# Normalising attention weights in the product that turns them, instead of before a transpose

## The chip, the cores and the metric

The kernel runs on one core of one Trainium2 chip. The metric is the device time of one execution in microseconds (us), from the median of several runs. A profile of one execution is shown beside it. Engine names in the profile are: PE for TensorE (PEld for its weight loads), DVE for VectorE, ACT for ScalarE, POOL for GpSimd, SP for SyncE.

## The reference

The reference is a two-layer model on 64 samples of 32 latent tokens with 256 channels, each sample with a context of 257 rows of 256 channels, all in float32. A layer is a cross attention to the context, a self attention and a feed-forward part (the first layer's is a mixture of 64 experts). The change touches the softmax of the two cross attentions alone. Cut to that:

```python
# layer 0: 16 heads, keys are the 257 context rows and the sample's own 32 tokens
sim  = einsum('bhid,bhjd->bhij', qn, kn)          # j runs over 289 keys
attn = softmax(where(mask, sim, -max), axis=-1)
out  = einsum('bhij,bhjd->bhid', attn, v)
x    = x + out.reshape(b, m, h * d) @ Wout + bout

# layer 1: 16 heads, keys are the 257 context rows
attn = softmax(einsum('bqhd,bkhd->bhqk', q, k), axis=-1)
y    = einsum('bhqk,bkhd->bqhd', attn, v)
x    = x + einsum('bqhd,hdo->bqo', y, wo) + bo
```

A softmax row is exp(s - max) divided by the sum of its exponentials. The division by the sum is what the change moves.

## The kernel before, in words

**Tiling.** The 2048 tokens are 16 tiles of 128 tokens, a tile holds four samples. In both cross attentions one sample has 32 tokens x 16 heads = 512 query rows, kept as four groups (g) of 128 rows on the partitions: `sim` is a tile of 128 x 4 x keys.

**Stages.** `before` runs the first cross attention, the self attention and the routing. `experts` runs the mixture. `after` runs the second cross attention, self attention and feed-forward part. In `before` and `after` a loop goes over the 64 samples, and one pass is called a slot here. The order of TensorE is the order of the program (`manual_schedule` for PE); the other engines are ordered by a scheduler that follows priorities, and `urgent` raises the priority of what is in it. In a slot the loop does one step of each of several samples, and generators (`tails`, `fronts`, `steps`) fill in the work of token tiles between them.

**First cross attention** (class CrossFirst). A slot does `keys(s + 2)`, `weigh(s)`, `norms(s + 2)`, `values(s)`, `spread(s + 2)`, `turn(s + 3)`, `scores(s + 2)` and `prepare(s + 4)`, with fill-in work at three places. `keys` multiplies 289 columns of the context by the key weights, 16 products with the name psA<-xT,wk. `norms` sums squares (line 1247, which reads the squares that ScalarE makes in line 1235). `scores` forms the query-key products (1287), multiplies them into `sim` (1297), adds the mask (1298) and calls `softmax_rows`: a maximum (193), four exponentials with their sums (195), a reciprocal of the sums (198), a scaled copy of the last 33 columns to a second place of the same tile (201), and the scaling of the four groups in place, two on ScalarE (206) and two on VectorE (208). The tile has three buffers, and behind the 289 columns it has room for that second copy.

**weigh.** `keyed` turns the weights: for each of three column groups of 128 keys it transposes the four row groups by TensorE into one PSUM bank (218) and copies the bank to SBUF (219), on whichever of ScalarE and VectorE the scheduler picks. `values` then multiplies the turned weights with the context (232, 242). Every transpose passes the 128x128 tile as the stationary operand and an identity from the constants tile `c` as the moving one, so the profile calls it psT<-c,sim.

**Second cross attention** (class CrossSecond). A slot does `weigh(s)`, `scores(s + 2)` and `values(s)`. `scores` has four products (psY<-xT,qk), each followed by a maximum (1387) and an exponential out of PSUM (1388), then a reciprocal (1391) and four scalings on VectorE (1393). `weigh` transposes two column groups and a third one in which key 256 is repeated 128 times (1405), and copies the banks out (1406). `values` multiplies with the context and adds the part of key 256 (1418).

**GpSimd's queue.** It has the two small copies into xT (1206, 1207) for `turn`, the scaling of queries (1151), the mask (1174, 1175), some additions, and the indirect transfers of the routing (665) and of the mixture's results (802). It works strictly in its own order.

Of the kernel before, what the change touches and what calls it, by code (L numbers as in the profile page):

```python
# [10 lines left out]
F32 = mybir.dt.float32  # L11
# [3 lines left out]
ALU = mybir.AluOpType  # L15
AX = mybir.AxisListType

P = 128
D = 256
S = 32  # L20
NB = P // S
J = 257
JK = J + S
# [76 lines left out]
class Kernel:  # L100
    def __init__(self, ctx, tc, a, out):
        self.ctx, self.tc, self.nc, self.a, self.out = ctx, tc, tc.nc, a, out
        self.nt = out.shape[0] // P
        self.nb = self.nt * NB
        self.const = ctx.enter_context(tc.tile_pool(name="const", bufs=1))
        self.ps = ctx.enter_context(tc.tile_pool(name="ps", bufs=8, space=bass.MemoryType.PSUM))
        self.small = ctx.enter_context(tc.tile_pool(name="small", bufs=4))
# [76 lines left out]
        nc.vector.tensor_tensor(xt, xt, ps, ALU.add)  # L184


    def softmax_rows(self, sim, n, twice=None):


        nc = self.nc  # L190
        mx = self.small.tile([P, 4], F32, name="mx")
        sm = self.small.tile([P, 4], F32, name="sm")
        nc.vector.tensor_reduce(mx, sim, AX.X, ALU.max, negate=True)  # L193
        for g in range(4):
            nc.scalar.activation(  # L195
                sim[:, g, :], sim[:, g, :], AF.Exp, bias=mx[:, g : g + 1], accum_out=sm[:, g : g + 1]
            )
        nc.vector.reciprocal(sm, sm)
        if twice is not None:
            m = twice.shape[2]  # L200
            nc.vector.tensor_tensor(
                twice, sim[:, :, n - m :], sm.unsqueeze(2).to_broadcast([P, 4, m]), ALU.mult
            )
        for g in range(4):
            if g % 2:
                nc.scalar.mul(sim[:, g, :], sim[:, g, :], sm[:, g : g + 1])
            else:
                nc.vector.tensor_scalar(sim[:, g, :], sim[:, g, :], sm[:, g : g + 1], None, ALU.mult)

    def keyed(self, sim, sizes):  # L210

        nc = self.nc
        at = self.atp.tile([P, len(sizes), 512], F32, name="at")
        k0 = 0
        for j, n in enumerate(sizes):
            ps = self.bank("psT")
            for g in range(4):
                nc.tensor.transpose(ps[:n, g * P : (g + 1) * P], sim[:, g, k0 : k0 + n], self.ident)
            nc.any.tensor_copy(at[:n, j, :], ps[:n, :])
            k0 += n  # L220
        return [at[:n, j, :] for j, n in enumerate(sizes)]
# [454 lines left out]
    def experts(self, ctx, slot, tails):  # L676
# [75 lines left out]
        for e in range(AHEAD):  # L752
            weigh(e)
# [17 lines left out]
        for e in range(E):  # L771
            weigh(e + AHEAD)
            fetch(e + 3)
            turn(e + 2)
            while (at - total + rest) * E < rest * e:
                next(side)
                at += 1
            inner(e + 1)
            outer(e)
            if e == AHEAD:  # L780
                self.after_weights()
            if e == 2 * AHEAD:
                self.ffnw = self.ffn_weights(self.w2)
# [319 lines left out]
class CrossFirst:  # L1103


    def __init__(self, k, kp):
        self.k, self.kp = k, kp
        self.own, self.held, self.cx, self.xT = {}, {}, {}, {}

    def given(self, wq, wk, gx, bx, gl, bl, gam, xl, xlT):  # L1110
        self.wq, self.wk_ = wq, wk
# [160 lines left out]
    def scores(self, s):  # L1272
        k = self.k
        nc = k.nc
        t, b = divmod(s, NB)
        _, _, qT, mb = self.own[t]
        _, _, kT, whole = self.held[s]
        sim = whole[:, :, :JK]
        for half in range(2):
            ps = [k.bank("psB") for _ in range(2)]  # L1280
            for u in range(2):
                for i in range(2):
                    for odd in range(2):
                        m = 2 * (2 * half + i) + u
                        q = PLACES[i].index(2 * u + odd)
                        r = slice(DH * odd, DH * odd + DH)
                        nc.tensor.matmul(
                            ps[i][q * S : (q + 1) * S, :JK],
                            lhsT=qT[r, m, b * S : (b + 1) * S],
                            rhs=kT[r, m, :],  # L1290
                            start=True,
                            stop=True,
                        )
            for i in range(2):
                g = 2 * half + i
                with k.urgent():
                    nc.vector.tensor_tensor(sim[:, g, :], ps[i][:, :JK], sim[:, g, :], ALU.mult)  # L1297
        nc.vector.tensor_tensor(sim, sim, mb[:, b, :].unsqueeze(1).to_broadcast([P, 4, JK]), ALU.add)
        k.softmax_rows(sim, JK, whole[:, :, 2 * P + 64 : 2 * P + 64 + S + 1])

    def weigh(self, s):

        k = self.k
        cx, c3, _, sim = self.held.pop(s)
        at = k.keyed(sim, [P, P, P])
        self.weights = at[:2], [cx[:, 0, :], cx[:, 1, :]], (at[2], c3)

    def values(self, s):
# [7 lines left out]
class CrossSecond:  # L1316
# [54 lines left out]
    def scores(self, s):  # L1371

        k, nc = self.k, self.k.nc
        t, b = divmod(s, NB)
        cx, xT = self.cx[s]
        qk = self.qk[t]
        sim = self.kp.tile([P, 4, J], F32, name="sim")
        mx = k.small.tile([P, 4], F32, name="mx")
        sm = k.small.tile([P, 4], F32, name="sm")
        for g in range(4):  # L1380
            ps = k.bank("psY")
            k.product(
                ps[:, :J],
                [qk[:, c, b, g * P : (g + 1) * P] for c in range(2)],
                [xT[:, c, :] for c in range(2)],
            )
            nc.vector.tensor_reduce(mx[:, g : g + 1], ps[:, :J], AX.X, ALU.max, negate=True)  # L1387
            nc.scalar.activation(  # L1388
                sim[:, g, :], ps[:, :J], AF.Exp, bias=mx[:, g : g + 1], accum_out=sm[:, g : g + 1]
            )  # L1390
        nc.vector.reciprocal(sm, sm)
        for g in range(4):
            nc.vector.tensor_scalar(sim[:, g, :], sim[:, g, :], sm[:, g : g + 1], None, ALU.mult)  # L1393
        self.held[s] = sim

    def weigh(self, s):

        k, nc = self.k, self.k.nc
        sim = self.held.pop(s)
        at = self.kp.tile([P, 3, 512], F32, name="at", bufs=1)  # L1400
        for j in range(3):
            ps = k.bank("psT")
            for g in range(4):
                x = sim[:, g, j * P : (j + 1) * P] if j < 2 else sim[:, g, J - 1 :].to_broadcast([P, P])
                nc.tensor.transpose(ps[:, g * P : (g + 1) * P], x, k.ident)  # L1405
            nc.any.tensor_copy(at[:, j, :], ps)
        self.at = at

# [93 lines left out]
```

## Time and profile before

| what | us |
|---|---|
| median of 3 timed runs | 2816.75 |
| lowest and highest of them | 2816.62, 2820.55 |
| the profiled execution's own time | 2814.6 |
| span of the profile, first to last instruction | 2812.4 |
| TensorE busy | 2650.2 |
| VectorE busy | 1730.6 |
| ScalarE busy | 1227.6 |
| GpSimd busy | 542.3 |

The busy times overlap, as the engines work side by side. A row of the profile's groups reads: line, engine, operation, what it writes and reads, shape, count, then the busy time of the group, the mean duration of one instruction in nanoseconds, and how long the engine sat idle before instructions of the group and what ended that. TensorE's matmuls are pipelined, so that the mean of one is longer than the distance from one start to the next. A row of the timeline has start, length, engine, line, operation and how many records it merges.

### The profile page before, as it was taken

The numbers are of one execution on the slowest core, as the hardware profiler recorded it, in microseconds if no ns is written. First come the engines' busy times: TensorE is split into PE (matmuls) and PEld (weight loads), VectorE is DVE, ScalarE is ACT, GpSimd is POOL, SyncE is SP. The second block draws the span as 40 slices with busy tenths as digits, with TensorE's granted clock in tenths as the row PEclk, the third lists the DMA queues.
The fourth block names the chain that finished last, engine by engine and source line by source line (L and its number), as shares of the span: only waits on it lengthen the run. The fifth ranks groups of instructions, "written<-read, shape, count | busy, mean of one in ns | idle before, by whom it ended". The sixth has DMA issues, their size and how long they took to land. (4 is left out here: it accounts for less than half of the span.)

```text
span 2812.4 us, 59421 instructions
## 1 busy us (share of the span) xinstructions
PE 2650.2 (94%) x23642; PEld 1823.7 (65%) x23642; DVE 1730.6 (62%) x4544; ACT 1227.6 (44%) x3463; POOL 542.3 (19%) x644
## 2 busy tenths in 40 slices
PE   6999999999999999999998799899999999999995
PEld 4566656665666566656665578677777777777763
DVE  6565656665666567656755433556666666666664
ACT  4555555555555555555553233333333333333331
POOL 3110122112211221122112200421222222121001
PEclk9999999999999999999998799999999999999997
DMA  7000011101100000000002587221212222221110
GB/s 263 27 16 14 18 31 33 31 18 31 32 30 18 27 26 22 18 19 19 17 5 82 182 268 229 80 71 48 61 48 58 52 55 59 50 57 47 33 33 7
DMA packets 136089, 157.05 MB, mean 56 GB/s; under 512 B 24025, under 2 KB 118980, under 8 KB 135813
## 3 DMA queue, kind: packets, MB, share of 16 engines
q1 hardware_dynamic: 114308, 119.65, 14.0%
q0 software_dynamic: 12288, 25.21, 3.4%
q10 hardware_dynamic: 9216, 8.39, 0.9%
q8 instruction: 187, 3.06, 0.5%
q14 instruction: 90, 0.73, 0.1%
HBM read 121.63 MB, written 37.75 MB: 57 GB/s over the span
## 5 line engine op out<-in xcount | busy, mean ns | idle before, releaser
L178 PE MATMUL psA<-xT,wk 128*128 128x289 f32 x2048 | 522.0, 410 | 17.9 <-issue 13.0
L178 PEld LDWEIGHTS psA<-xT,wk 128*128 128x128 f32 x2048 | 384.0, 190 | 150.1 <-issue 46.5
L802 POOL DMA_INDIRECT y<-oute,idx x128 | 131.5, 1027 | 657.4 <-DVE x L813 466.8
L232 PE MATMUL psY<-at,cx 128*128 128x512 f32 x512 | 238.1, 608 | 0.0
L178 PE MATMUL psA<-at,cx 128*128 128x512 f32 x512 | 233.5, 599 | 0.0
L178 PE MATMUL psY<-xT,qk 128*128 128x257 f32 x1024 | 233.5, 380 | 0.0
L178 PEld LDWEIGHTS psY<-xT,qk 128*128 128x128 f32 x1024 | 189.8, 190 | 25.1
L1388 ACT ACTIVATE sim<-psY,mx 128x257 f32<-128x257 f32 x256 | 120.8, 476 | 148.6 <-DVE mx L1387 147.7
L232 PEld LDWEIGHTS psY<-at,cx 128*128 128x128 f32 x512 | 92.8, 191 | 123.1 <-issue 99.7
L195 ACT ACTIVATE sim<-sim,mx 128x289 f32<-128x289 f32 x256 | 135.5, 532 | 64.4 <-DVE mx L193 64.3
L178 PEld LDWEIGHTS psA<-at,cx 128*128 128x128 f32 x512 | 93.4, 190 | 96.5 <-issue 83.3
L1235 ACT ACTIVATE sq<-kT 128x1156 f32<-128x1156 f32 x128 | 148.6, 1161 | 12.6 <-DVE kT L1232 11.4
L244 ACT COPY yT<-psY 128x512 f32<-128x512 f32 x128 | 68.7, 589 | 189.8 <-PE psY L242 189.8
L1297 DVE TENSOR_TENSOR sim<-psB,sim 128x289 f32<-128x289 f32 x256 | 100.7, 451 | 81.5 <-PE psA L178 37.9
L1230 ACT COPY kT<-psA 128x289 f32<-128x289 f32 x256 | 99.2, 388 | 115.7 <-PE psA L178 113.6
L665 POOL DMA_INDIRECT buf<-z,fi x128 | 126.4, 987 | 96.3 <-DVE fi L662 54.0
L1232 DVE COPY kT<-psA 128x289 f32<-128x289 f32 x256 | 114.3, 451 | 40.0 <-PE psA L178 39.9
L178 PE MATMUL psY<-yT,wv 128*64 128x128 f32 x2048 | 127.9, 277 | 7.3 <-DVE yT L1418 7.3
L1387 DVE TENSOR_REDUCE mx<-psY 128x1 f32<-128x257 f32 x256 | 101.0, 418 | 52.6 <-PE psY L178 47.5
L178 PEld LDWEIGHTS psY<-yT,wv 128*64 128x64 f32 x2048 | 116.6, 138 | 16.3 <-DVE yT L1418 11.2
L184 DVE TENSOR_TENSOR x<-x,psY 128x256 f32<-128x256 f32 (+1 forms) x80 | 29.2, 365 | 156.4 <-PE psY L178 154.8
L178 PE MATMUL psY<-wo,oT 128*128 128x128 f32 (+1 forms) x768 | 124.2, 315 | 0.0
(254 smaller groups left out, 5005.7 us busy)
## 6 DMA issues: line engine op xcount, KB each, us to landing
cx<-in_ctx SPq DMA_DIRECT2D x128, 256.0 KB
we<-in_m_ew SPq DMA_DIRECT2D x64, 384.0 KB
xT<-in_ctxT SPq DMA_DIRECT2D x64, 257.0 KB
buf<-zero SPq DMA_DIRECT2D x32, 256.0 KB
be<-buf SPq DMA_DIRECT2D x64, 128.0 KB
oute<-oe ACTq DMA_DIRECT2D x64, 128.0 KB
mu<-in_mask SPq DMA_DIRECT2D x16, 128.5 KB
x<-in_x SPq DMA_DIRECT2D x16, 128.0 KB
```

The lines of the kernel that those rows point to most:

```text
L178: self.nc.tensor.matmul(ps, lhsT=lhs[i], rhs=rhs[i], start=(i == 0), stop=(i == n - 1))
L195: nc.scalar.activation(sim[:, g, :], sim[:, g, :], AF.Exp, bias=mx[:, g : g + 1], accum_out=sm[:, g : g + 1])
L232: nc.tensor.matmul(ps[kc], lhsT=values[i][:, kc * P : (kc + 1) * P], rhs=at[i], start=(i == 0), stop=(i == n - 1 and tail is None),)
L244: nc.any.tensor_copy(yT[:, kc, :, b * S : (b + 1) * S], ps[kc].rearrange("p (h i) -> p h i", h=H))
L665: d = nc.gpsimd.indirect_dma_start(out=self.buf[:, :], out_offset=bass.IndirectOffsetOnAxis(ap=fi[:, k : k + 1], axis=0), in_=z[:, 0, :], ...
L802: nc.gpsimd.indirect_dma_start(out=y, out_offset=None, in_=self.oute[:, :], in_offset=bass.IndirectOffsetOnAxis(ap=self.idx[:, t, k : k + ...
L1230: nc.scalar.copy(kT[:, p, :], ps[:, :JK])
L1232: nc.vector.tensor_copy(kT[:, p, :], ps[:, :JK])
L1235: nc.scalar.activation(sq[p // 4], kT[:, p - 3 : p + 1, :], AF.Square)
L1297: nc.vector.tensor_tensor(sim[:, g, :], ps[i][:, :JK], sim[:, g, :], ALU.mult)
L1387: nc.vector.tensor_reduce(mx[:, g : g + 1], ps[:, :J], AX.X, ALU.max, negate=True)
L1388: nc.scalar.activation(sim[:, g, :], ps[:, :J], AF.Exp, bias=mx[:, g : g + 1], accum_out=sm[:, g : g + 1])
```

## The change

`softmax_rows` and the second `scores` no longer scale `sim`. It keeps the bare exponentials. A new helper, `diagonal`, takes the reciprocals of the four sums and forms a tile of 128 x 4 x 128: for each row group, the identity with row r multiplied by that row's reciprocal. `keyed` and `weigh` then turn a 128x128 tile x of `sim` by an ordinary product with the diagonal as the moving operand, which gives x turned, with each column scaled by its row's reciprocal. The second copy of the last 33 columns is made unscaled and by GpSimd, behind the exponentials. The diagonal of each sample is kept from `scores` to `weigh` in a dictionary or in the held pair. Both sides of the diff have the same number of turns, PSUM banks and copies out of PSUM.

```diff
-    def softmax_rows(self, sim, n, twice=None):
+    def softmax_rows(self, pool, sim, n, twice=None):
...
+        if twice is not None:
+            nc.gpsimd.tensor_copy(twice, sim[:, :, n - twice.shape[2] :])
+        return self.diagonal(pool, sm)
+
+    def diagonal(self, pool, sm):
+
+        nc = self.nc
         nc.vector.reciprocal(sm, sm)
-        if twice is not None:
-            m = twice.shape[2]
-            nc.vector.tensor_tensor(
-                twice, sim[:, :, n - m :], sm.unsqueeze(2).to_broadcast([P, 4, m]), ALU.mult
-            )
-        for g in range(4):
-            if g % 2:
-                nc.scalar.mul(sim[:, g, :], sim[:, g, :], sm[:, g : g + 1])
-            else:
-                nc.vector.tensor_scalar(sim[:, g, :], sim[:, g, :], sm[:, g : g + 1], None, ALU.mult)
-
-    def keyed(self, sim, sizes):
+        dg = pool.tile([P, 4, P], F32, name="dg", bufs=2)
+        nc.vector.tensor_tensor(
+            dg, self.ident.unsqueeze(1).to_broadcast([P, 4, P]), sm.unsqueeze(2).to_broadcast([P, 4, P]), ALU.mult
+        )
+        return dg
+
+    def turned(self, ps, x, dg):
+
+        self.nc.tensor.matmul(ps, lhsT=x, rhs=dg, start=True, stop=True)
+
+    def keyed(self, sim, dg, sizes):
...
-                nc.tensor.transpose(ps[:n, g * P : (g + 1) * P], sim[:, g, k0 : k0 + n], self.ident)
+                self.turned(ps[:n, g * P : (g + 1) * P], sim[:, g, k0 : k0 + n], dg[:, g, :])
...
-        k.softmax_rows(sim, JK, whole[:, :, 2 * P + 64 : 2 * P + 64 + S + 1])
+        dg = k.softmax_rows(self.kp, sim, JK, whole[:, :, 2 * P + 64 : 2 * P + 64 + S + 1])
+        self.ready[s] = dg
...
-        at = k.keyed(sim, [P, P, P])
+        at = k.keyed(sim, self.ready.pop(s), [P, P, P])
...
-        nc.vector.reciprocal(sm, sm)
-        for g in range(4):
-            nc.vector.tensor_scalar(sim[:, g, :], sim[:, g, :], sm[:, g : g + 1], None, ALU.mult)
-        self.held[s] = sim
+        self.held[s] = sim, k.diagonal(self.kp, sm)
...
-        sim = self.held.pop(s)
+        sim, dg = self.held.pop(s)
...
-                nc.tensor.transpose(ps[:, g * P : (g + 1) * P], x, k.ident)
+                k.turned(ps[:, g * P : (g + 1) * P], x, dg[:, g, :])
```

More of the change, by code (lines that the diff above doesn't have):

```diff
@@ L1107, in __init__ @@
         self.k, self.kp = k, kp
-        self.own, self.held, self.cx, self.xT = {}, {}, {}, {}
+        self.own, self.held, self.cx, self.xT, self.ready = {}, {}, {}, {}, {}
     def given(self, wq, wk, gx, bx, gl, bl, gam, xl, xlT):
```

## The prediction

> **What bounds the kernel now.** I read the page's busy shares first, then the busy time by stage, then what TensorE waits for inside the two stages that the change touches, and last the timeline of TensorE, for the price of one turn. The page has TensorE at 94% of the span, ahead of everything else:
>
> ```profile
> PE 2650.2 (94%) x23642; PEld 1823.7 (65%) x23642; DVE 1730.6 (62%) x4544; ACT 1227.6 (44%) x3463; POOL 542.3 (19%) x644
> ```
>
> A share over the whole span can mislead, so here is the busy time by stage. The first cross attention turns its weights (line 218) from 61.8 to 1513.5 us, the second (line 1405) from 1800.1 to 2746.8 us.
>
> ```profile
> core 0: us, PE busy (x) PEld busy (x) DVE busy (x) ACT busy (x) POOL busy (x), PEclk, DMA share, GB/s
> 60.00:760.00 700.00, 676.67 (x5505) 427.89 (x5505) 446.72 (x1213) 377.63 (x1031) 130.47 (x171) 1.00 0.10 29
> 760.00:1460.00 700.00, 680.48 (x6012) 434.56 (x6003) 456.96 (x1295) 374.50 (x1044) 142.00 (x187) 1.00 0.07 20
> 1790.00:2740.00 950.00, 918.70 (x8997) 688.26 (x8996) 620.47 (x1440) 336.21 (x996) 189.63 (x184) 1.00 0.19 52
> ```
>
> The reader is to see three things. TensorE is busy 97% of both stages, at full granted clock. What is left idle is 23.3 + 19.5 = 43 us in the first and 31 us in the second, 74 us together. VectorE stands at 65% and ScalarE at 35 to 54%, so time taken off those two is not time off the end. The waits of TensorE inside the stages (us in total, times, longest) say the same; the first two lines are of the first stage, the others of the second:
>
> ```profile
> PE psA L178 <- issue: 12.1, 28, 1.0
> PE psB L1247 <- ACT sq L1235: 10.3, 14, 2.0
> ...
> PE psA L178 <- ACT zT L162: 15.7, 27, 0.7
> PE psY L178 <- DVE yT L1418: 7.1, 14, 0.9
> ```
>
> None of them ends on the scaling of weights (lines 201, 206, 208, 1393). The chain of the removed work is already hidden; what the change puts on TensorE is not.
>
> **What a turn costs on TensorE.** The groups by shape give the number of records:
>
> ```profile
> L1405 PE MATMUL psT<-c,sim 128*128 128x128 f32 x768 | 95.7, 275 | 0.0
> L218 PE MATMUL psT<-c,sim 128*128 128x128 f32 x768 | 94.6, 273 | 1.0 <-issue 0.9
> L178 PE MATMUL psA<-zT,wq 128*128 128x128 f32 x512 | 61.3, 278 | 11.8 <-ACT zT L162 9.7 <-DVE zT L162 2.1
> ```
>
> Each stage turns 64 samples x 3 column groups x 4 row groups = 768 tiles, and has 768 records: one per transpose. The query product of the second stage issues 16 token tiles x 2 x 4 x 2 = 256 products and has 512 records: a float32 product is two records, each with its own weight load. The mean of one (275, 278) is a latency in a pipe; the rate is read from start to start:
>
> ```profile
> 1954.30 3.84 PE L178 MATMUL psA<-zT,wq 128*128 128x128 f32 x32 [0.73 <-ACT zT L162]
> 1957.98 1.47 PE L1405 MATMUL psT<-c,sim 128*128 128x128 f32 x12
> 1959.29 3.64 PE L178 MATMUL psY<-xT,qk 128*128 128x257 f32 x16
> ```
>
> ```profile
> 1690.43 1.06 PE L178 MATMUL psA<-beT,we 128*128 128x128 f32 x8
> 1691.32 0.60 PE L178 MATMUL psY<-we,eact 128*128 128x256 f32 x2
> ```
>
> Twelve transposes take 1959.29 - 1957.98 = 1.31 us, 109 ns each. Records of a product with the same 128x128 tiles, every one with fresh weights, take 3.68/32 = 115 ns in the first place and 0.89/8 = 111 ns in the second. A turn by product is therefore 222 to 230 ns; I take 2 x 112 = 224, as the tight run of eight is nearest to twelve turns issued together. The loss per turn is 224 - 109 = 115 ns (113 to 121).
>
> Here a rule of the Trainium skill is to be weighed. "TensorE: Matmul & The Clock Gate", in its Terms, gives the transpose mode as four times faster for FP32, and "Perfetto Trace Analysis", under Transposes, asks for a real transpose instead of a standard matmul. Both speak against this change. By the factor of four a transpose would be 224/4 = 56 ns, the loss 168 ns a turn and 1536 x 0.168 = 258 us in all. The rows say 109 ns, a factor of 2.05, so the loss is smaller than the rule makes it. I go by the rows.
>
> **The change part by part, and the sum.**
> - Turns: 1536 more records. 1536 x 0.115 = 176.6 us of TensorE (173.6 to 185.9), all in stages where it has next to nothing to hide in. A slot of one sample, now 1451.7/63 = 23.0 us in the first stage and 946.7/63 = 15.0 us in the second, gets 1.38 us longer. Their weight loads are the loads of those records and lie beside the products as they do for zT,wq.
> - Scaling removed. VectorE loses 80.3 us (line 1393), 45.0 (208) and 18.9 (201); ScalarE loses 66.8 (206). On the path this is worth nothing but what it takes from TensorE's waits.
>
> ```profile
> L1393 DVE TENSOR_SCALAR sim<-sim,sm 128x257 f32<-128x257 f32 x256 | 80.3, 366 | 2.2
> L201 DVE TENSOR_TENSOR sim<-sim,sm 128x132 f32<-128x132 f32 x64 | 18.9, 295 | 1.3
> L309 DVE TENSOR_TENSOR e<-e,smh 128x512 f32<-128x512 f32 x32 | 21.9, 685 | 0.1
> L206 ACT ACTIVATE sim<-sim,sm 128x289 f32<-128x289 f32 x128 | 66.8, 536 | 19.8 <-DVE sim L201 19.8
> L1206 POOL COPY xT<-lnT 128x64 f32<-128x64 f32 x64 | 19.7, 309 | 377.6 <-PE psA L178 235.5 <-ACT lnT L162 142.1
> ```
>
> - Diagonal added: one 128x512 product with broadcast operands on VectorE per sample and stage, 128 in all. Line 309 is the same form: 685 ns, so 87.7 us (with two broadcast sources I allow 650 to 900 ns, which moves nothing on TensorE). VectorE nets -56.5 us. A turn waits now for the reciprocal and this one instruction, where it waited for four scalings (4 x 0.366 us), so the weights are ready earlier. The slack is large anyway: scores(s + 2) is issued right behind weigh(s) or in its slot, and its own turns come more than a slot later. If that cover were gone, each sample would lose the 0.69 us, 88 us in all.
> - Copy on GpSimd, first stage only: 132 elements, between the 309 ns of a 64-element copy and the 487 ns of a 128-element two-input operation, say 0.4 us, 64 times, 26 us of an engine at 19%. It waits for the last exponential, and behind it on that queue stand the copies into xT (1206, 1207), the scatters (665) and the query scaling (1151). The xT copies wait for the end of the same keys product anyway; at 778 us they are done 13 us before their reader. The third column group of the turns waits for this copy, a slot after it was issued. I cost it at nothing.
> - Two more PSUM writes per turn, no more evictions: three per sample as before, now 0.9 us apart and not 0.44, which eases them.
> - Given back: the 10.3 us wait for line 1235 comes directly behind the turns, with 0.74 us at a time, under the 1.38 us that are put in front of it; I count 10. Of the other 33 us idle in the first stage about 5 for the freed ScalarE. In the second stage the waits are for a copy between two neighbouring products, and the turns do not stand there: nothing. Together 15.
>
> Sum: 176.6 - 15 = 161.6. The profiled execution took 2814.6 us (span 2812.4), so 2976.2; the median of the timed runs lies 2.15 higher, so 2978.
>
> **The rivals.**
> 1. Turns cost nothing (faster). If a turn by product streamed like a transpose, at about 109 ns, TensorE would stay where it is and the 123 us taken off VectorE and ScalarE would shorten its waits. Their cap is the 74 us; by the same sorting as above some 20 us, so 2797. It decides from 109 + 20/1.536 = 122 ns per turn downwards. Against it: every float32 product in the profile has two records, and only the transposes have one. Chance 3%, and 1% for landing within 0.2%, which is about what a measurement of this kernel can tell from no change.
> 2. Much given back. If half of the 74 us idle and the small stalls inside the busy time vanish, 173.6 - 45 = 129, so 2945; the whole 74 would give 2916. For it: VectorE's long instructions hold PSUM banks in the first stage. Against: the waits for "issue" and copies come from the hand-written order, not from full engines. 6%.
> 3. GpSimd late (slower still). At a token tile's start its queue is held for 20.5 us (scatters from 737.2, query scaling, mask, to 757.7). A slot is 23 us, so a copy queued behind all of it just arrives in time; a few us more and TensorE waits, at most 16 x 5 = 80 us on top: 3058. 5%.
> 4. The main case, 2955 to 3003: 85%.
>
> The range 2945 to 3003 takes the turns from 113 to 121 ns and the given-back time from 45 to 0. Slower by over 0.2% is 96%.
>
> **What would show it.** TensorE's records rise by 1536 to 25178; the rows of the turns show 1536 records each, 24 in about 2.7 us from start to start. TensorE's busy time rises to about 2820 at a share of 95%; VectorE falls to about 1674, ScalarE to about 1161, GpSimd rises to about 568. The wait of line 1247 for line 1235 all but vanishes. I am wrong if the turns keep 768 records each, if a record costs clearly under 105 ns, or if turns wait for the diagonal or for GpSimd's copy.

## The result, and the profile after

The changed kernel takes 2966.68 us (median of 4 runs, 2963.59 to 2971.22) against 2816.78 us: 149.9 us more, a ratio of 1.053 with a 95% interval of 1.0509 to 1.0551. The forecast was 2978 in a range of 2945 to 3003. The kernel before itself took about 2817 us in two of the four sets of runs told of here and about 2751 in the two others, so every kernel below is compared with the one before in its own set.

The page of the changed kernel begins, engine by engine, with busy time, share and number of instructions:

```profile
PE 2820.5 (95%) x25178; PEld 2007.1 (68%) x25178; DVE 1617.1 (55%) x4099; ACT 1274.6 (43%) x3460; POOL 572.2 (19%) x708
```

TensorE has 1536 records more than before (25178 against 23642) and 170.3 us more busy time. The count is what two records per turn make of it, and the busy time is close to the 176.6 us of the forecast. VectorE and ScalarE did not land where the forecast had them, 1674 and 1161; that is taken up below. The groups and the timeline give the turn:

```profile
L214 PE MATMUL psT<-dg,sim 128*128 128x128 f32 x3072 | 367.2, 276 | 2.9 <-issue 2.8
```

```profile
829.24 2.84 PE L214 MATMUL psT<-dg,sim 128*128 128x128 f32 x24
831.92 0.38 PE L161 MATMUL psT<-c,z 128*128 128x128 f32 x2
```

Twenty-four records take 831.92 - 829.24 = 2.68 us, 112 ns each, 223 ns a turn. Before, twelve transposes took 1.31 us. The lengths of the two stages, from first to last turn, come from the rows of the tile for each stage (minimum, median and maximum duration, then first and last start):

```profile
L214 PE MATMUL psT<-dg,sim x1536: 269/275/417, 62.3 to 1579.4; 128*128 128x128 f32 x192
L214 PE MATMUL psT<-dg,sim x1536: 272/275/422, 1863.7 to 2898.3; 128*128 128x128 f32 x192
```

The kernel before has these:

```profile
L218 PE MATMUL psT<-c,sim x768: 270/273/314, 62.0 to 1513.6; 128*128 128x128 f32 x192
L1405 PE MATMUL psT<-c,sim x768: 272/273/421, 1800.3 to 2746.9; 128*128 128x128 f32 x192
```

The first stage grew from 1451.6 to 1517.1 us, by 65.5, the second from 946.6 to 1034.6, by 88.0. The spans differ by 151.9. The second stage pays the forecast 768 x 0.115 = 88.3 us in full. The first gives 22.8 us of it back.

TensorE's waits in the changed kernel, first stage and then second, show where that came from, and what took its place:

```profile
PE psB L1293 <- issue: 18.9, 30, 1.7
PE psB L1293 <- ACT qTf L1173: 6.7, 15, 1.8
...
PE psB L1253 <- ACT sq L1241: 0.6, 1, 0.6
...
PE psA L178 <- ACT zT L162: 15.7, 27, 0.7
PE psY L178 <- DVE yT L1422: 9.0, 14, 0.7
```

The wait for line 1241 (1235 before) fell from 10.3 us to 0.6, and the waits for "issue" ahead of psA products and of line 161's transposes (12.1 + 3.9) are gone. Instead 18.9 us for "issue" stand ahead of the score products (1293; 3.1 before, as line 1287), and 2.8 ahead of the turns. All waits of TensorE in this stage together fell from 47.1 to 30.8 us, so 16 of the 22.8 us come from them. In the second stage the waits are within 2 us of those before.

Last, the copies of turned weights out of PSUM, first of the changed kernel, then of the kernel before (lines 225 and 1410 were 219 and 1406):

```profile
L1410 ACT COPY at<-psT x191: 567/585/589, 1865.6 to 2898.6; 128x512 f32<-128x512 f32 x191
...
L225 ACT COPY at<-psT x118: 562/585/619, 66.1 to 1579.7; 128x512 f32<-128x512 f32 x118
L225 DVE COPY at<-psT x74: 650/684/692, 65.6 to 1551.6; 128x512 f32<-128x512 f32 x74
```

```profile
L219 DVE COPY at<-psT x137: 652/681/693, 65.4 to 1513.5; 128x512 f32<-128x512 f32 x137
...
L1406 ACT COPY at<-psT x117: 564/587/604, 1801.4 to 2747.4; 128x512 f32<-128x512 f32 x117
L1406 DVE COPY at<-psT x75: 679/692/693, 1819.8 to 2737.6; 128x512 f32<-128x512 f32 x75
```

These copies go to whichever engine the scheduler picks. With ScalarE rid of its scalings, it moved 137 of them there (117 + 55 before, 191 + 118 now).

### The profile page after: what moved, and what is told of

The parts are those of the page before. It is cut to its first block, busy times and chain, and to the rows that moved or that the text cites. A ratio compares the mean times of both kernels' runs of the same rounds, so it can differ in the third digit from the quotient of the medians.

```text
span 2964.3 us, 62179 instructions
## 1 busy us (share of the span) xinstructions
PE 2820.5 (95%) x25178; PEld 2007.1 (68%) x25178; DVE 1617.1 (55%) x4099; ACT 1274.6 (43%) x3460; POOL 572.2 (19%) x708
## 4 chain that ended last, share of the span: by engine, by line
PE 86%; DVE 6%; ACT 4%; issue 2%; DMA 2%; SPq 0%; POOL 0%; POOLq 0%; DVEq 0%; ACTq 0%
PE psA L178 34%; PE psY L178 18%; PE psT L214 12%; PE psY L238 8%; PE psB L1253 2%; PE psB L1293 2%; PE psY L248 2%; PE psA L1355 1%; PE psY L328 1%; PE psB L178 1%; PE psT L161 1%; DMA be<-buf 1%; PE psR L1274 1%; DVE st L141 1%; ACT sim L1275 1%
## 5 line engine op out<-in xcount | busy, mean ns | idle before, releaser
L214 PEld LDWEIGHTS psT<-dg,sim 128*128 128x128 f32 x3072 | 363.4, 193 | 12.6 <-issue 3.9
L214 PE MATMUL psT<-dg,sim 128*128 128x128 f32 x3072 | 367.2, 276 | 2.9 <-issue 2.8
L1410 ACT COPY at<-psT 128x512 f32<-128x512 f32 x191 | 110.2, 584 | 176.0 <-PE psT L214 118.7
L1241 ACT ACTIVATE sq<-kT 128x1156 f32<-128x1156 f32 x128 | 149.0, 1164 | 12.4 <-DVE kT L1238 10.3
L199 POOL COPY sim<-sim 128x132 f32<-128x132 f32 x64 | 22.5, 351 | 666.4 <-ACT sim L195 411.6
```

What stands on the lines that cost most here:

```text
L214: self.nc.tensor.matmul(ps, lhsT=x, rhs=dg, start=True, stop=True)
L1241: nc.scalar.activation(sq[p // 4], kT[:, p - 3 : p + 1, :], AF.Square)
```

## The experiments

Theory A: the cost is TensorE's second record per turn, and the rest of the change, with the engines that it frees, is worth little. Rivals: the freed engines pay back a visible part; or the diagonal or GpSimd's copy costs the time.

**Turns alone, and the rest alone.** `turns_only` is the kernel before with

```diff
-nc.tensor.transpose(ps[:n, ...], sim[:, g, k0 : k0 + n], self.ident)
+nc.tensor.matmul(ps[:n, ...], lhsT=sim[:, g, k0 : k0 + n], rhs=self.ident, start=True, stop=True)
```

and the same in the second stage. `rest_only` is the changed kernel with

```diff
-self.nc.tensor.matmul(ps, lhsT=x, rhs=dg, start=True, stop=True)
+self.nc.tensor.transpose(ps, x, self.ident)
```

so that its weights are never divided by their sums.

> The kernel before with its 1536 turns made by products with the identity; the scalings stay where they were. Theory (the price is TensorE's two records per turn, the freed VectorE and ScalarE work is worth little): 2817 + 176.6 for the turns - about 10 for the wait behind the longer turns = 2983, at most 25 us above the changed kernel (2967). Rival (the time given back came from the scalings that were removed): nothing is given back here, so 2993 or more. Second rival (the diagonal, not the product, costs the time): near 2817.

> The changed kernel with the turns made by transposes again: diagonals are formed and not used, so the weights are left unscaled. Theory: the rest of the change is worth 0 to 20 us, so 2797 to 2817, and the turns by product cost 150 to 170 us on top of it. Rival (the freed engines shorten TensorE's waits much): 2790 or less. Rival (a diagonal or GpSimd's copy is late): over 2817.

`turns_only` took 2925.72 us against 2751.25, +174.5 (ratio 1.0634, 1.0613 to 1.0655, so 169 to 180). `rest_only` took 2747.6, -3.7 (0.9983, 0.9975 to 0.9991). The turns alone, with every scaling in place, cost all of it and the diagonal costs nothing; the rest of the change is a gain of about 4 us. The forecast of 2983 for `turns_only` was +166 on 2817, and the measured +174.5 is between it and the first rival's +176; its interval holds the rival and not the forecast. To decide between them, the first stage of `turns_only` is compared with that of `first_only`, the next experiment:

```profile
L218 PE MATMUL psT<-c,sim x1536: 271/275/276, 63.8 to 1533.2; 128*128 128x128 f32 x192
```

It lasted 1469.4 us with every scaling in place. `first_only`, which has none of them in this stage, needed 1470.4.

**One stage at a time.** `first_only` keeps the second cross attention as before, `second_only` the first.

> The change in the first cross attention alone. Theory: 768 turns x 0.115 = 88.3 us, and all the time given back is in this stage, where TensorE had 43 us of waits: from the two traces the stage grew by 65 us, so 2882. Rival (the given-back time is spread over both stages): 2817 + 76 = 2893.

> The change in the second cross attention alone. Theory: 768 x 0.115 = 88.3 us with nothing given back, so 2904 to 2906. Rival (given-back time is spread over both stages): 2893.

In the same set `first_only` took 2830.07, +78.8 (1.0283, 1.0262 to 1.0305), where the theory had +65 (read from the two first profiles) and the rival +76. `second_only` took 2846.91, +95.7 (1.0345, 1.0324 to 1.0366), where they had +87 to 89 and +76. Neither came out as the theory had it. Together they are 174.5. The stages by their turns:

```profile
L214 PE MATMUL psT<-dg,sim x1536: 271/275/276, 62.7 to 1533.1; 128*128 128x128 f32 x192
```

```profile
L222 PE MATMUL psT<-dg,sim x1536: 272/275/422, 1739.7 to 2774.9; 128*128 128x128 f32 x192
L232 PE MATMUL psT<-c,sim x768: 271/273/273, 63.6 to 1456.7; 128*128 128x128 f32 x192
```

The first fence is the first stage of `first_only`, 1470.4 us. The second is the second stage of `second_only`, 1035.2 us, and its unchanged first stage, 1393.1 us. So the first stage grew by 77.3, and 11 us of the 88.3 are given back there, not 23. As `turns_only` gives back as much (76.3 grown), the freed engines have no part in it. The unchanged first stage is 58 us shorter here than in the first profile of the kernel before (1451.6), and that is most of the 65.5 us between the two levels of the kernel before. The second stage is within 3 us the same in every profile with transposes once per turn.

The +95.7 of `second_only` is 7 us more than its stage grew. They lie behind the last turn: from there to the end it takes 72.8 us, `first_only` 65.4. First `first_only`, then `second_only`, in the self attention there:

```profile
2779.82 1.29 PE L1056 MATMUL psB<-kTl,qf 32*32 32x32 f32 x128
2781.04 3.70 PE L178 MATMUL psA<-wl,zT 128*128 128x512 f32 x8
```

```profile
2793.46 0.31 PE L1064 MATMUL psB<-kTl,qf 32*32 32x32 f32 x2 [2.03 <-issue]
2793.70 6.49 PE L178 MATMUL psA<-wl,zT 128*128 128x512 f32 x8
```

TensorE stands for 2.0 us inside a run of small products, twice in this part. The eight products behind the first stop take 6.49 us instead of 3.70, and the clock granted over the part is 0.69 against 0.78. `turns_only`, and below `before_twice` and `second_r`, have two such stops there, of 1.7 to 2.6 us, and 72 to 74 us in all; the other kernels have none and 62 to 67. What brings them about stays open. They are no part of what a turn costs. Without them `turns_only` is at about +167, where the theory had +166.

What is different in the first stage shows in the busy time of the engines in steps of 3 us beside one token tile's scatters. First `before_again` below (the kernel before in a set at 2817 us), then `second_only`, whose first stage is the same:

```profile
744.00:747.00 3.00, 2.97 (x39) 1.32 (x38) 0.87 (x2) 2.20 (x6) 2.39 (x3) 1.00 0.62 221
747.00:750.00 3.00, 1.79 (x6) 0.69 (x5) 0.41 (x1) 0.00 (x0) 2.39 (x4) 1.00 0.26 93
750.00:753.00 3.00, 2.63 (x9) 1.74 (x10) 1.47 (x5) 0.37 (x1) 0.31 (x2) 1.00 0.11 40
```

```profile
728.00:731.00 3.00, 3.00 (x43) 1.61 (x42) 1.36 (x3) 1.82 (x6) 2.30 (x3) 1.00 0.44 152
731.00:734.00 3.00, 3.00 (x14) 2.35 (x13) 3.00 (x7) 0.98 (x4) 2.48 (x2) 1.00 0.25 90
734.00:737.00 3.00, 3.00 (x14) 2.32 (x13) 2.22 (x4) 1.55 (x6) 2.99 (x5) 1.00 0.11 40
```

The columns are the stretch and its length, the busy time of PE, PEld, DVE, ACT and POOL, the granted clock, the share of the DMA engines and their GB/s. In the first, VectorE and ScalarE all but stop for some 3 us, and TensorE does six records, at full clock. In the second, the same work runs through. This is the stall of the runs at 2817 us, once per token tile.

TensorE's waits in the first stage of `first_only` show what the stall had put there in the changed kernel:

```profile
PE psB L1293 <- ACT qTf L1173: 6.7, 15, 1.9
PE psA L178 <- ACT xT L1211: 2.0, 3, 0.9
PE psB L1253 <- ACT sq L1241: 0.6, 1, 0.6
```

The 18.9 us for "issue" are not among them; it is the same code. With the stall this stage lasted 1517.1 us, without it 1470.4: 47 us of stall are left in the changed kernel, of 58 in the one before. The longer slots hide 12 us of it.

**Transposes twice, products twice, and both kernels again.** `before_twice` and `after_twice` issue every turn twice into the same place; `before_again` and `after_again` are the two kernels as they are.

```diff
 nc.tensor.transpose(ps[:n, ...], sim[:, g, k0 : k0 + n], self.ident)
+nc.tensor.transpose(ps[:n, ...], sim[:, g, k0 : k0 + n], self.ident)
```

> The kernel before itself, with a profile, on the chip of these runs. Both theories: no difference from the kernel before on this chip. Its first stage tells whether the stall once per token tile, seen beside the scatters in the two first profiles, is the chip's or the code's: with it the stage lasts about 1450 us, without it about 1393.

> The changed kernel itself. Theory (the two earlier parts add up: +78.8 for the first stage, +95.7 for the second; or +174.5 for the turns and -3.7 for the rest): 171 to 175 us above the kernel before, a ratio of 1.062 to 1.064, if the stall per token tile is absent; with the stall, part of it is hidden again and the difference is about 150. Rival (the engines freed and the longer slots give back 15 us or more whatever the chip): 150 to 160 in both cases.

> The kernel before with each of the 1536 transposes issued twice into the same place. Theory (a transpose costs 109 ns of TensorE, nothing hides it): 1536 x 0.109 = 167.4 us more, less up to 10 given back. Rival (by the rule that a transpose is four times as fast as a product, 56 ns): 86 us more.

> The changed kernel with each turn by product issued twice. Theory (a turn by product is 2 x 112 = 224 ns of TensorE): 344 us above the changed kernel, so about 517 above the kernel before. Rival (weight loads of neighbouring records limit it, so that a second product on the same tile comes cheaper, or the PSUM bank is held too long and costs more): under 300 or over 380 above the changed kernel.

This set was at the higher level: before 2817.71, `before_again` 2815.99 (0.9995, 0.9986 to 1.0003). `after_again` took 2971.06, +153.4 (1.0535, 1.0514 to 1.0555), as the theory has it with the stall present, though the rival for `after_again` allowed that too. `before_twice` took 2970.2, +152.5 (1.0539, 1.0521 to 1.0557), of which 7.5 us are the two stops behind the last turn (72.6 us there, 65.1 in `before_again`). The expectation was 157 to 167, the rule's 86 is out. `after_twice` took 3302.63, 331.6 above `after_again`, 216 ns a turn, a little under the 344 expected: its second stage grew by 171.9 us, 224 ns a turn as forecast, its first by 159.5.

`before_twice` is the useful one for the give-back, as it frees neither VectorE nor ScalarE:

```profile
L218 PE MATMUL psT<-c,sim x768: 269/273/417, 66.3 to 1583.0; 128*128 128x128 f32 x192
...
L1406 PE MATMUL psT<-c,sim x768: 272/273/421, 1867.1 to 2896.1; 128*128 128x128 f32 x192
```

First `before_again`, then `after_again`, first stage:

```profile
L218 PE MATMUL psT<-c,sim x768: 270/273/317, 65.7 to 1518.5; 128*128 128x128 f32 x192
L214 PE MATMUL psT<-dg,sim x1536: 269/275/422, 64.0 to 1587.1; 128*128 128x128 f32 x192
```

In `before_again` the stage is 1452.8 us long. In `before_twice` it is 1516.7, 63.9 more, where 768 transposes of 109 ns are 83.7 and the second stage grew by 79.9 (949.1 to 1029.0): 16 to 20 us are given back, with every scaling in place. `after_again` has it at 1523.1 us, 70.3 more of 88.3: 18 given back. So it is the longer slot that gives back, not the freed engines.

**Without the scatters.** Both kernels with the eight indirect transfers of line 665 per token tile left out, so that the experts read zeros.

```diff
-        for k in range(TOPK):
-            d = nc.gpsimd.indirect_dma_start(
-                out=self.buf[:, :],
...
```

> The kernel before without the scatters of the routing (line 665), so that the experts read zeros. First theory (the stall of all engines once per token tile in the first stage comes with the scatters): the first stage falls from about 1452 us to about 1393, the whole by 55 to 65 us on a chip that shows the stall, by under 8 on one that does not. Rival (the stall is of something else): under 10 us less on either chip.

> The changed kernel without the scatters of the routing. First theory (the 23 us given back against 1536 x 0.115 = 176.6 are part of the stall beside the scatters): with the stall gone in both, 170 to 175 us above the kernel before without scatters. Rival (longer slots and freed engines give the time back): 150 to 160 above it, as with the scatters.

This set came at the lower level (before 2752.03), where the stall is absent anyway, so the pair does not test what ties the stall to the scatters. `before_noscat` took 2742.6, -9.4, over the 8 expected for such a case. Its first stage, 1389.9 us, is not shorter than the same code's with the scatters in this set (1388.0 in `second_r` below); 7 us less lie between the stages (276.8 against 283.7), where the experts read zeros. `after_noscat` took 2905.98, 163.4 above it, which neither 170 to 175 nor 150 to 160 had. The 170 to 175 were built on +95.7 and +174.5, which both hold the 7 us behind the last turn. Its first stage ran from 61.9 to 1532.5 us against 64.0 to 1453.9: 80.7 more, 8 given back. With `first_only` (11) and `turns_only` (12) that makes 8 to 12 us given back without the stall, against 16 to 23 with it. So the change costs about 163 us without the stall (measured without the scatters) and 150 to 153 with it.

**One record per turn.** Here both operands of the turns are declared float32r, another type of four bytes per number; what it does to the accuracy was not measured. `second_r` does it in the second stage on top of `second_only`. `both_r` does it in both, with the first stage's exponentials in a tile of their own with two buffers, where `sim` had three.

```diff
-self.nc.tensor.matmul(ps, lhsT=x, rhs=dg, start=True, stop=True)
+self.nc.tensor.matmul(ps, lhsT=x.bitcast(F32R), rhs=dg.bitcast(F32R), start=True, stop=True)
```

> The change in the second cross attention alone, with both operands of the turns declared float32r, so that [...] a turn may be one record. Theory (time goes with the number of records and 109 to 112 ns is the rate of a record): one record per turn, no more than 5 us from the kernel before. Rival (such a record passes the array once and takes about half, 56 ns): 768 x 0.053 = 41 us less than before. Rival (still two records): 85 to 95 us more.

> The whole change with float32r operands in the turns of both stages; the exponentials of the first stage go to a tile of their own (two buffers) [...]. Theory (one record, 109 to 112 ns): the kernel before, less the 4 us that the rest of the change was worth, so -8 to +4 us. Rival (a record at 56 ns): 1536 x 0.053 = 81 us less, plus what a shorter slot uncovers. Rival (two records): 150 to 175 us more.

```profile
L215 PE MATMUL psT<-dg,ex x768: 272/275/441, 64.2 to 1451.8; 128*128 128x128 f32 x192
...
L215 PE MATMUL psT<-dg,sim x768: 272/274/625, 1734.7 to 2684.9; 128*128 128x128 f32 x192
```

One record per turn, and the time is back: `both_r` took 2756.21, +4.2 (1.0008, 0.9998 to 1.0019), and `second_r` 2763.41, +11.4 (1.0035, 1.0028 to 1.0043), which is more than the 5 that the theory allowed. The 7 us between the two are again the stops behind the last turn (73.8 us there in `second_r`, 66.6 in `both_r`). The diagonal, GpSimd's copy and the product are all still there, and the second record is gone. A turn did not become cheaper than a transpose, as the rival had it. None of the kernels that do the whole computation beats the one before.

## Why the prediction was right or wrong

- **Two records per turn at 112 ns, 115 ns lost per turn: right.** The count is 1536 a stage. 112 ns is the measured distance, the second stage grew by 88.0 of 88.3 us, and `both_r`, with one record, loses the cost.
- **The rule of the factor of four: rightly set aside.** It was the Trainium skill's, of "TensorE: Matmul & The Clock Gate", Terms (the transpose mode four times faster for FP32); the estimate from it was a cost of 258 us, and 150 were measured. In the second stage, which gives next to nothing back, `before_twice` prices a transpose at 79.9/768 = 104 ns, not at 56.
- **Nothing waits for the diagonal or for GpSimd's copy: right.** The row of the turns in the changed kernel has 2.9 us of idle time, none of it for VectorE or GpSimd; `rest_only` is not slower than before. The rival of a late GpSimd did not come about.
- **Given back: 15 us forecast, 23 measured in the first stage.** This term was mis-sized, and it is most of the distance from 2978 to 2967. The 10 us for the wait on the squares came as worked out (10.3 to 0.6), but that size belongs to one execution: the same wait is 5.7 us in `before_again` and 3.1 in the unchanged first stage of `second_only`. The 5 us for a freed ScalarE have no support: `before_twice` gives back 16 to 20 us with nothing freed, and `turns_only` as much as `first_only`. What the working did not have is the stall beside the scatters, of which the longer slot hides 12 us. I had read its waits ("issue", 12.1 us) as a consequence of the order written by hand; where the stall is absent, so are they. Without the stall the cost is about 163 us, next to the forecast's 161.6, but its terms do not hold there either: the wait on the squares gives 2.5 (3.1 to 0.6) and the freed ScalarE nothing. That this sum fits is luck. In `first_only` TensorE's waits are 9.5 us against 13.0 in the same stage of `second_only`, so most of the 11 us came back inside TensorE's busy time, and where stays open.
- **VectorE 1674 and ScalarE 1161 us: wrong, without effect.** Measured are 1617.1 and 1274.6. The sum of the removed and added instructions left out that the copies out of PSUM choose their engine; 137 of them moved to ScalarE at about 0.585 us, which is 80 of the 114 us missing there. The rest is not worked out.
- **The wait on line 1235 vanishes: right; but "issue" ahead of line 1293 took a place (18.9 us)** that the forecast did not name. It is the stall again.
- **"Two more PSUM writes per turn": one more.** A turn was one record and is two. Nothing hung on it.

## What to carry to other kernels

On an engine that is busy 97% of a stage, count records, not operations: folding a scaling into a float32 product that replaces a transpose doubled the records of the turn, and work taken off engines with room to spare paid 4 us for 175. Ask of every edit whose busy time it moves where, and take freed time on a side engine as worth nothing until a wait names it. What came back here came from the longer slots. Before a wait is entered as time that comes back, see whether other executions of the same code have it too.

## What the runs showed of the hardware

A record with fresh 128x128 weights and up to 128 moving columns takes 109 to 132 ns from start to start whatever it does: a transpose 109, half of a float32 product 111 to 115, a float32r product 114 to 132 (twelve in 1.37 us in one place of `both_r`, in 1.59 in another). In the kernel before, even products with 65 moving columns take as much:

```profile
810.94 0.66 PE L178 MATMUL psA<-gw,zT 128*128 128x65 f32 x4
811.44 2.00 PE L178 MATMUL psY<-wo,oT 128*128 128x128 f32 x16
```

Four records of 65 columns take 0.50 us, 125 ns each, sixteen of 128 columns 1.84 us, 115 ns each. Halving the moving columns does not help. Halving the columns of the weights does, as another product of the kernel before shows, whose weights are 64 columns of `wv`:

```profile
2752.76 3.71 PE L178 MATMUL psY<-yT,wv 128*64 128x128 f32 x62 [0.23 <-DVE yT L1418]
2756.40 3.72 PE L178 MATMUL psY<-wo,oT 128*128 128x256 f32 x16
```

Sixty-two records with 128 moving columns, each with its own weight load, take 3.64 us, 59 ns each. That points to the weight load as the floor of such a record. Half the weights also means half the rows of output, and no run here varied the load alone, so it is argued, not shown.

The stall of about 4 us per token tile in the first stage (94.3 us a tile in the runs at 2817, 90.0 in `second_only`) stops VectorE, ScalarE and mostly TensorE at full granted clock. It sits beside the scatters, and comes in some sets of runs of the same program and not in others. The sets of `before_again` (with it) and of `before_noscat` (without) are recorded for a chip of the same number, so neither the code nor the chip alone decides. What causes it stays open: the one pair of kernels that would tell was run where it did not occur.
